# LayerNorm's inverse roots from GpSimd to ScalarE, and one of two outer products of the input weights from GpSimd to VectorE

## The chip, the cores and the metric

The kernel runs on one core of a Trainium2 chip. The metric is the device time of one execution in microseconds. Engines are called as the profile calls them: PE is TensorE's matmul and PEld its weight load, DVE is VectorE, ACT is ScalarE, POOL is GpSimd, SP is SyncE, which issues the DMAs. Each engine has its own list of instructions and takes them in the order in which the built program has them.

## What is computed

Two transformer blocks on x of 16 x 512 x 256, each with a modulated LayerNorm ahead of its two parts. The first block has a layer with fast weights and a low-rank MLP, the second has windowed attention and a channel mix.

```python
def _layernorm(x, axis=-1, eps=1e-05):
    m = jnp.mean(x, axis=axis, keepdims=True)
    v = jnp.var(x, axis=axis, keepdims=True)
    return (x - m) / jnp.sqrt(v + eps)

h = _layernorm(x, axis=-1) * (1 + ca) + sa      # and three more of this kind
```

The layer with fast weights runs over chunks of 16 tokens, one after the other. For each batch row and head it carries two matrices of 4 x 16, W_in and W_out, from chunk to chunk:

```python
def attn(q, k, v):
    s = jnp.einsum('bqhd,bkhd->bhqk', q, k) / jnp.sqrt(jnp.asarray(q.shape[-1], q.dtype))
    p = jax.nn.softmax(s, axis=-1)
    return jnp.einsum('bhqk,bkhd->bqhd', p, v)

for _ in range(2):
    g_out = -attn(W_in, k_t, v_t)
    g_in = -attn(W_out, v_t, k_t)
    W_in = W_in - lr_in * g_in
    W_out = W_out - lr_out * g_out
```

## The kernel before

The batch is cut in two halves of 8 rows, and time in 8 stretches of 64 tokens: 16 units u, whose half is u % 2. Each unit goes through five streams: `prepare` (norm a, projections, convolutions), `chain` (the recurrence, 4 chunks of 16 tokens), `mlp` (norm b), `attend` (norm c) and `mix` (norm d). They are Python generators. `timetable` (L1122) gives each of their steps a due time in units, and the steps of all units are issued in the order of those times, so that the recurrence of two units, one of each half, runs beside the other streams of earlier and later units. From what is issued the tile framework makes the order of each engine's list and the waits between engines.

`recur` (L587) is one chunk of the recurrence: 128 partitions are 8 batch rows by 16 heads. The products are made in full, as 128 x 1024 elements, on one engine, and then summed by VectorE:

- `scores` (L523) multiplies tokens and weights (sc_k, sc_q, sc_v, VectorE) and sums over d. The weights lie in `fw`, one bank of PSUM; the tokens (tok) lie in SBUF.
- `exp_tokens` (L537) takes maximum and exponential, `over_tokens` (L545) divides by the sum and multiplies with the rate (e_k, e_v, L549).
- `outer` (L530) multiplies such weights of tokens with v or k: pd_o, pd_kv and pd_i, all on POOL at L534. Both operands and the result are in SBUF. `big` (L520) gives the results one ring of five buffers.
- `total` (L634) sums a product over tokens: do and di (L636).

The two inner steps of the reference are folded together: W_in is read for the first g_out, then both gradients of W_in come from W_out at two stages, sv with 2R rows (L640 to L644). Their weights are e_v. The two products of these with k are pd_i (L647); the first sum, di0, goes into W_in at L649, which the second sc_k needs; the second, di1, follows at L653, behind that sc_k and its exponential.

The running sum over tokens, W_out at each token, is the scan at L631 (within and pd_kv, both in SBUF). Other VectorE instructions that read two operands from SBUF are mix (L1033), ov (L679), mx with mg (L900), lr (L573), and off (L353).

`norm_T` (L340) is the LayerNorm of one unit; it is called 64 times, 16 for each of a, b, c and d. VectorE takes mean and variance (mv, L348), POOL adds epsilon (L350) and raises to the power of -0.5 (L351), VectorE makes off = -mean times that root (L353), ACT applies both (xn, L359), PE transposes, and ACT applies the modulation on the way out of PSUM (L367).

ACT's table of functions is that with exponential and logarithm, except in bursts of Silu, Gelu and Tanh, around which `run` (L220) loads tables. Elsewhere `inverse_root` (L201) makes roots on ACT as Ln and Exp.

Of the kernel before, what the change touches and what calls it, by code (L numbers as in the profile page):

```python
# [12 lines left out]
AF = mybir.ActivationFunctionType  # L13
ALU = mybir.AluOpType
# [3 lines left out]
P = 128  # L18
B, T, C = 16, 512, 256
H, D, R = 16, 16, 4  # L20
CH = 16
TB = 64
HB = 8
NR = HB // 2
# [10 lines left out]
EPS = 1e-5  # L35
# [60 lines left out]
def adaln_blocks(ctx: ExitStack, tc: tile.TileContext, a: dict, out: bass.AP):  # L96
    nc = tc.nc
    mul, add, sub = ALU.mult, ALU.add, ALU.subtract
# [9 lines left out]
    def ctile(shape, name):  # L108
        return const.tile(shape, F32, tag=name, name=name)

    def bank(name):
        return ps.tile([P, 512], F32, tag="bank", name=name)
# [75 lines left out]
    nc.vector.tensor_copy(ident_bf, ident)  # L188

    w_proj = ctile([P, 2, 2, C], "w_proj")  # L190
    mhalf = ctile([P, 1], "mhalf")
    nc.vector.memset(mhalf, -0.5)

    def hold(dst, n):

# [144 lines left out]
    def norm_T(x, layer, which, b0, tag, hT):  # L340


        m = mods[layer]
        mv = work.tile([P, NR, 2], F32, tag=f"mv_{tag[0]}", name=f"mv_{tag}", bufs=1)
        for r in range(NR):
            st = work.tile([P, 6], F32, tag="st", name=f"st_{tag}_{r}", bufs=4)
            nc.vector.bn_stats(st, x[:, r, :])
            nc.vector.bn_aggr(mv[:, r, :], st)  # L348
        rs = work.tile([P, NR], F32, tag=f"rs_{tag[0]}", name=f"rs_{tag}", bufs=1)
        nc.gpsimd.tensor_scalar(rs, mv[:, :, 1], EPS, None, add)  # L350
        nc.gpsimd.tensor_tensor(rs, rs, mhalf.to_broadcast([P, NR]), ALU.pow)  # L351
        off = work.tile([P, NR], F32, tag=f"off_{tag[0]}", name=f"off_{tag}", bufs=1)
        nc.vector.scalar_tensor_tensor(off, mv[:, :, 0], -1.0, rs, mul, mul)  # L353
        for r2 in range(NR // 2):
            pt = bank(f"pt_{tag}_{r2}")
            for n in range(2):
                r = 2 * r2 + n
                xn = work.tile([P, C], F32, tag="xn", name=f"xn_{tag}_{r}", bufs=2)
                nc.scalar.activation(xn, x[:, r, :], AF.Identity, scale=rs[:, r : r + 1], bias=off[:, r : r + 1])  # L359
                for k in range(2):  # L360
                    nc.tensor.transpose(pt[:, (2 * n + k) * P : (2 * n + k + 1) * P], xn[:, k * P : (k + 1) * P], ident)
            for n in range(2):
                for k in range(2):
                    for e in range(2):
                        b = 4 * r2 + 2 * n + e
                        col = (2 * n + k) * P + e * TB
                        nc.scalar.activation(  # L367
                            hT[:, k, b, :],
                            pt[:, col : col + TB],
                            AF.Identity,  # L370
                            scale=m[:, 2 * which + 1, k, b0 + b : b0 + b + 1],
                            bias=m[:, 2 * which, k, b0 + b : b0 + b + 1],
                        )
            yield
# [19 lines left out]
    def place(u):  # L394

        return u % NH, u // NH
# [120 lines left out]
    def small(half, name, n):  # L517
        return rec.tile([P, n], F32, tag=f"s{n}_{half}", name=name, bufs={XW: 5, 2 * XW: 3}.get(n, 4))

    def big(half, name):  # L520
        return rec.tile([P, R * D * CH], F32, tag="prod", name=name, bufs=5)
# [5 lines left out]
        engine.tensor_tensor(pr, tok.unsqueeze(1).to_broadcast(every), w.unsqueeze(2).to_broadcast(every), mul)  # L527
        nc.vector.tensor_reduce(dst, pr, AX.X, add)  # L528

    def outer(half, engine, hid, tok, tag):  # L530

        pr = big(half, f"pd_{tag}").rearrange("p (r d t) -> p r d t", r=R, d=D)
        every = [P, R, D, CH]
        engine.tensor_tensor(pr, hid.unsqueeze(2).to_broadcast(every), tok.unsqueeze(1).to_broadcast(every), mul)  # L534
        return pr

    def exp_tokens(half, s, n, mx, tag):  # L537
# [7 lines left out]
    def over_tokens(half, e, n, rate, sm):  # L545

        nc.vector.tensor_reduce(sm, e, AX.X, add)
        nc.vector.reciprocal(sm, sm)
        nc.vector.scalar_tensor_tensor(e, e, rate, sm.unsqueeze(2).to_broadcast([P, n, CH]), mul, mul)  # L549
        return e  # L550
# [36 lines left out]
    def recur(u, pc, c, s):  # L587

        half = place(u)[0]
        f = fws[half]  # L590
        tag = f"{u}_{pc}_{c}"
        cs = slice(c * CH, (c + 1) * CH)
        k_dt, v_dt, q_dt, lr = s["k"][:, :, cs], s["v"][:, :, cs], s["q"][:, :, cs], s["lr"]
        lr_in, lr_out = lr[:, 0, c * CH : c * CH + 1], lr[:, 1, c * CH : c * CH + 1]
        tok = rec.tile([P, 3, CH, D], F32, tag=f"tok_{half}", name=f"tok{tag}", bufs=1)
        for n, x in enumerate((k_dt, q_dt, v_dt)):
            nc.scalar.copy(tok[:, n], x.rearrange("p d t -> p t d"))  # L597
        k, q, v = (tok[:, n] for n in range(3))
        w_in, w_out, w_outs = f["w_in"], f["w_out"], f["w_outs"]

        sc = small(half, f"scs{tag}", 2 * XW).rearrange("p (r t) -> p r t", r=R)
        scores(half, nc.vector, k, w_in, sc[:, :, :CH], f"k{tag}")
        scores(half, nc.vector, q, w_in, sc[:, :, CH:], f"q{tag}")
        late[half]()
        p_out = exp_tokens(half, sc[:, :, :CH], R, f["mx_k"], f"k{tag}")


        mx = f["hid"]
        nc.vector.tensor_reduce(mx, sc.rearrange("p r t -> p t r"), AX.X, ALU.max)
        hid = small(half, f"hid{tag}", R * 2 * CH).rearrange("p (r t) -> p r t", r=R)  # L610
        every = [P, R, 2 * CH]
        nc.vector.tensor_tensor(hid, sc, mx.unsqueeze(1).to_broadcast(every), sub)
        nc.scalar.activation(hid, hid, AF.Exp)
        yield
        d_out = outer(half, nc.gpsimd, over_tokens(half, p_out, R, lr_out, f["sm_k"]), v_dt, f"o1{tag}")

        sm = f["hid"][:, :CH]
        kh, qh = hid[:, :, :CH], hid[:, :, CH:]
        nc.vector.tensor_reduce(sm, kh.rearrange("p r t -> p t r"), AX.X, add)
        nc.vector.tensor_reduce(s["sum"][:, cs], qh.rearrange("p r t -> p t r"), AX.X, add)  # L620
        nc.vector.reciprocal(sm, sm)
        nc.vector.tensor_tensor(sm, sm, lr[:, 1, cs], mul)
        nc.vector.tensor_tensor(kh, kh, sm.unsqueeze(1).to_broadcast([P, R, CH]), mul)  # L623


        kv = outer(half, nc.gpsimd, kh, v_dt, f"kv{tag}")
        yield
        nc.vector.tensor_tensor(kv[:, :, :, 0], kv[:, :, :, 0], w_out, add)
        upto = kv
        flat = kv.rearrange("p r d t -> p (r d t)")  # L630
        nc.vector.tensor_tensor_scan(flat, within, flat, 0.0, mul, add)  # L631
        nc.vector.tensor_copy(w_outs[:, :R], upto[:, :, :, CH - 1])  # L632

        def total(pr, name):  # L634
            t = small(half, f"{name}{tag}", XW).rearrange("p (r d) -> p r d", r=R)
            nc.vector.tensor_reduce(t, pr, AX.X, add)  # L636
            return t


        sv = small(half, f"sv{tag}", 2 * XW).rearrange("p (r t) -> p r t", t=CH)  # L640
        nc.vector.tensor_tensor(w_outs[:, R:], total(d_out, "do1"), w_outs[:, :R], add)
        for n in range(2):
            scores(half, nc.vector, v, w_outs[:, n * R : (n + 1) * R], sv[:, n * R : (n + 1) * R], f"v{n}{tag}")
        p_in = exp_tokens(half, sv, 2 * R, f["mx_v"], f"v{tag}")  # L644
        yield
        p_in = over_tokens(half, p_in, 2 * R, lr_in, f["sm_v"])
        d_in = [outer(half, nc.gpsimd, p_in[:, n * R : (n + 1) * R], k_dt, f"i{n}{tag}") for n in range(2)]  # L647
        yield
        nc.vector.tensor_tensor(w_in, total(d_in[0], "di0"), w_in, add)  # L649
        sk = small(half, f"sk{tag}", XW).rearrange("p (r t) -> p r t", t=CH)  # L650
        scores(half, nc.vector, k, w_in, sk, f"k2{tag}")
        p_out = exp_tokens(half, sk, R, f["mx_k"], f"k2{tag}")
        nc.vector.tensor_tensor(w_in, total(d_in[1], "di1"), w_in, add)  # L653
        yield
        d_out = outer(half, nc.gpsimd, over_tokens(half, p_out, R, lr_out, f["sm_k"]), v_dt, f"o2{tag}")
        yield
        late[half] = lambda: nc.vector.tensor_tensor(w_out, total(d_out, "do2"), w_outs[:, R:], add)


        po = upto  # L660
        nc.gpsimd.tensor_tensor(po, qh.unsqueeze(2).to_broadcast([P, R, D, CH]), upto, mul)  # L661
        nc.gpsimd.tensor_tensor(po[:, :2], po[:, :2], po[:, 2:], add)
        nc.gpsimd.tensor_tensor(q_dt, po[:, 0], po[:, 1], add)
# [531 lines left out]
```

## Time and profile before

| | |
|---|---|
| time before, median of 3 runs | 3226.88 us (3222.9 to 3235.52) |
| time of the profiled execution | 3231.29 us |
| its span, first to last instruction | 3229.5 us |
| granted TensorE clock, mean | 0.822 |
| busy VectorE, TensorE, ACT, POOL | 2395.3, 2385.4, 1783.6, 1673.0 us |
| pd_i on POOL (L534) | 128 of 2369 ns |
| pd_o, pd_kv on POOL (L534) | 128 of 2358 ns, 64 of 2366 ns |
| inverse roots on POOL (L350, L351) | 64 of 0.23 us, 64 of 1.04 us |
| first and last start of a pd_i | 153.3 and 2956.6 us |
| table loads on ACT | 232 of 1283 ns |

A group's row in the profile has line, engine, operation, output and inputs by the program's names, their sizes, and a count; then busy us and the mean ns of one; then the engine's idle time just before them, and what ended it. A row of waits says who waited for whom: us in total, how often, and the longest. A row of one line's instructions gives minimum, median and maximum duration. What is idle is not in itself lost: it matters where the waiting engine is the one that others then wait for.

### The profile page before, as it was taken

The page shows a single profiled execution, that of the slowest core. Times are in us where ns is not written, and L with a number is a line of the kernel's source. Part 1 is how long each engine was busy: PE and PEld are TensorE (multiplying, and loading weights), DVE is VectorE, ACT ScalarE, POOL GpSimd, SP SyncE. Part 2 cuts the span into 40 slices and gives each one's busy share as a digit, 9 for nine tenths or more (in the row PEclk, how much of TensorE's full clock was granted, in tenths as well). Part 3 has the DMA queues.
Part 4 walks back from the last instruction along what each step waited for, and adds up shares of the span by engine and source line. Part 5 has one row for each costly group of instructions (what it writes and reads, how often), then busy time and mean ns, then how long its engine had stood idle before and what let it go on. Part 6 is the DMA issues. An engine that isn't in the chain of part 4 may idle for free.

```text
span 3229.5 us, 47324 instructions
## 1 busy us (share of the span) xinstructions
PE 2385.4 (74%) x17232; PEld 1452.9 (45%) x17232; DVE 2395.3 (74%) x4513; ACT 1783.6 (55%) x3748; POOL 1673.0 (52%) x1575
## 2 busy tenths in 40 slices
PE   3540156868787776887788887889787888788996
PEld 2210123444444454554445554555445555555664
DVE  1688787878787787778888888888888878774221
ACT  1761354556665745565564666566664655445543
POOL 0245556556556655555556564555555655654112
PEclk7775676878797887888888798979888887879998
DMA  5420112132314132131313223230402212122010
GB/s 151 94 58 13 47 37 67 31 73 55 80 36 94 32 83 54 51 83 33 88 27 72 69 59 75 51 83 27 100 21 72 62 51 56 45 52 60 17 28 27
DMA packets 439307, 186.46 MB, mean 58 GB/s; under 512 B 323937, under 2 KB 413090, under 8 KB 439074
## 3 DMA queue, kind: packets, MB, share of 16 engines
q1 hardware_dynamic: 439074, 183.44, 23.2%
q8 instruction: 135, 2.21, 0.3%
q14 instruction: 98, 0.80, 0.1%
HBM read 116.66 MB, written 66.72 MB: 57 GB/s over the span
## 4 chain that ended last, share of the span: by engine, by line
DVE 33%; PE 22%; POOL 20%; ACT 12%; issue 8%; DMA 4%; SPq 1%; POOLq 0%; DVEq 0%; ACTq 0%
POOL pd_o L534 5%; POOL pd_i L534 4%; DVE pd_kv L631 4%; DVE sc_v L527 3%; POOL pd_kv L534 3%; DVE sv L528 3%; DVE do L636 2%; PE st L873 2%; DVE di L636 2%; DVE sc_k L527 2%; DVE pp L460 2%; PE pproj L1005 2%; DMA oT<-o 2%; DVE scs L528 2%; DVE mx L889 1%
## 5 line engine op out<-in xcount | busy, mean ns | idle before, releaser
L534 POOL TENSOR_TENSOR pd_o<-e_k,dt_v 128x1024 f32<-128x1024 f32 x128 | 301.0, 2358 | 171.4 <-DVE e_k L549 171.3
L534 POOL TENSOR_TENSOR pd_i<-e_v,dt_k 128x1024 f32<-128x1024 f32 x128 | 298.4, 2369 | 43.4 <-DVE e_v L549 43.4
L708 PE MATMUL pwo<-w_WoT,oT 128*128 128x256 f32 x256 | 106.6, 576 | 223.0 <-POOL oT L701 201.8
L873 PE MATMUL st<-qs,keys 32*128 32x128 f32 x2048 | 191.3, 336 | 71.7 <-DVE yT L983 29.0
L661 POOL TENSOR_TENSOR pd_kv<-hid,pd_kv 128x1024 f32<-128x1024 f32 x64 | 150.3, 2349 | 165.6 <-DVE fw L632 141.6
L873 PE MATMUL sc<-keys,qs 32*128 32x128 f32 x2048 | 183.1, 326 | 71.7 <-DVE mx L889 41.7
L636 DVE TENSOR_REDUCE do<-pd_o 128x64 f32<-128x1024 f32 x126 | 152.3, 1213 | 102.5 <-POOL pd_o L534 102.5
L636 DVE TENSOR_REDUCE di<-pd_i 128x64 f32<-128x1024 f32 x128 | 155.1, 1214 | 88.3 <-POOL pd_i L534 88.3
L873 PEld LDWEIGHTS st<-qs,keys 32*128 32x128 f32 x2048 | 160.5, 226 | 132.2 <-DVE mx L889 32.4
L873 PEld LDWEIGHTS sc<-keys,qs 32*128 32x128 f32 x2048 | 148.0, 216 | 141.9 <-DVE mx L889 58.8
L889 DVE TENSOR_REDUCE mx<-sc 128x4 f32<-128x512 f32 x256 | 168.2, 679 | 26.2 <-PE sc L870 26.2
L708 PEld LDWEIGHTS pwo<-w_WoT,oT 128*128 128x128 f32 x256 | 68.4, 287 | 250.7 <-POOL oT L701 218.3
L534 POOL TENSOR_TENSOR pd_kv<-hid,dt_v 128x1024 f32<-128x1024 f32 x64 | 151.4, 2366 | 54.7 <-DVE hid L623 50.0
L926 ACT ACTIVATE pT<-st 128x512 f32<-128x512 f32 x256 | 135.3, 605 | 73.7 <-PE st L870 73.4
L631 DVE TENSOR_TENSOR_SCAN pd_kv<-within,pd_kv 128x1024 f32<-128x1024 bf16 x64 | 174.4, 2725 | 0.9
L527 DVE TENSOR_TENSOR sc_k<-tok,fw 128x1024 f32<-128x1024 f32 x128 | 155.4, 1214 | 14.8 <-ACT tok L597 13.5
L527 DVE TENSOR_TENSOR sc_v<-tok,fw 128x1024 f32<-128x1024 f32 x128 | 150.3, 1215 | 1.6
L224 ACT ACT_TABLE_LOAD x111 | 142.4, 1283 | 14.3 <-PE ph L736 7.6
L528 DVE TENSOR_REDUCE sv<-sc_v 128x64 f32<-128x1024 f32 x128 | 149.6, 1209 | 0.0
L736 PE MATMUL ph<-PT,w_v 64*128 64x512 f32 x256 | 111.1, 669 | 38.0 <-ACT z L224 27.8
L1005 PE MATMUL pproj<-w_proj,yT 128*128 128x256 f32 x512 | 122.9, 386 | 11.2 <-DVE yT L983 9.3
L197 PE MATMUL pmx<-w_w_attnT,blocks 128*128 128x384 f32 x256 | 118.5, 593 | 13.4 <-ACT hp L367 9.4
(251 smaller groups left out, 6827.7 us busy)
## 6 DMA issues: line engine op xcount, KB each, us to landing
values<-values SPq DMA_DIRECT2D x56, 256.0 KB
gate_a<-gates SPq DMA_DIRECT2D x64, 128.0 KB
xa<-in_x_dram SPq DMA_DIRECT2D x32, 256.0 KB
x<-in_x_dram SPq DMA_DIRECT2D x32, 256.0 KB
gate_c<-gates SPq DMA_DIRECT2D x64, 128.0 KB
gate_d<-gates SPq DMA_DIRECT2D x64, 128.0 KB
q<-y SPq DMA_DIRECT2D x64, 128.0 KB
dt_q<-q SPq DMA_DIRECT2D x32, 256.0 KB
```

Of the source, the lines that this page charges most:

```text
L224: ins = nc.scalar.activation(*args[0], **args[1])
L527: engine.tensor_tensor(pr, tok.unsqueeze(1).to_broadcast(every), w.unsqueeze(2).to_broadcast(every), mul)
L528: nc.vector.tensor_reduce(dst, pr, AX.X, add)
L534: engine.tensor_tensor(pr, hid.unsqueeze(2).to_broadcast(every), tok.unsqueeze(1).to_broadcast(every), mul)
L631: nc.vector.tensor_tensor_scan(flat, within, flat, 0.0, mul, add)
L636: nc.vector.tensor_reduce(t, pr, AX.X, add)
L661: nc.gpsimd.tensor_tensor(po, qh.unsqueeze(2).to_broadcast([P, R, D, CH]), upto, mul)
L708: nc.tensor.matmul(po[:, n * C : (n + 1) * C], lhsT=pair(oT, k, 2 * b2 + n), rhs=w_o[:, k, :], start=k == 0, stop=k == 1,)
L873: nc.tensor.matmul(dst, lhsT=lhsT, rhs=rhs, start=start, stop=False, skip_group_check=True)
L889: nc.vector.tensor_reduce(mx[:, j], sc[j].rearrange("p (s k) -> p s k", s=NS), AX.X, ALU.max)
L926: nc.scalar.activation(pT[j], st[j], AF.Exp)
L1005: nc.tensor.matmul(po[:, n * C : (n + 1) * C], lhsT=yT[:, k2, par].rearrange("p e t -> p (e t)"), rhs=w_proj[:, k2, par, :], start=k2 == 0 ...
```

## The change

Two things are changed. In `norm_T` the two POOL instructions of each norm, sum with epsilon and power, become two ACT instructions: Ln with epsilon as a bias, and Exp with the factor -0.5. The constant tile mhalf (-0.5) becomes eps. And `outer` takes a list of engines, between which it could divide the R rows of a product. All its callers give one engine. Of the two pd_i the first, whose sum is di0, is now given to VectorE, and the second stays on POOL. Everything else computes as before, but the order of the engines' lists is made anew for the whole program. In it the first pd_i stands directly behind its e_v on VectorE's list in 27 of 64 chunks, and one instruction later in 37.

```diff
-    mhalf = ctile([P, 1], "mhalf")
-    nc.vector.memset(mhalf, -0.5)
+    eps = ctile([P, 1], "eps")
+    nc.vector.memset(eps, EPS)
...
-        nc.gpsimd.tensor_scalar(rs, mv[:, :, 1], EPS, None, add)
-        nc.gpsimd.tensor_tensor(rs, rs, mhalf.to_broadcast([P, NR]), ALU.pow)
+        nc.scalar.activation(rs, mv[:, :, 1], AF.Ln, bias=eps)
+        nc.scalar.activation(rs, rs, AF.Exp, scale=-0.5)
...
-    def outer(half, engine, hid, tok, tag):
+    def outer(half, engines, hid, tok, tag):
 
         pr = big(half, f"pd_{tag}").rearrange("p (r d t) -> p r d t", r=R, d=D)
-        every = [P, R, D, CH]
-        engine.tensor_tensor(pr, hid.unsqueeze(2).to_broadcast(every), tok.unsqueeze(1).to_broadcast(every), mul)
+        n = R // len(engines)
+        every = [P, n, D, CH]
+        for k, engine in enumerate(engines):
+            part = slice(k * n, (k + 1) * n)
+            engine.tensor_tensor(
+                pr[:, part], hid[:, part].unsqueeze(2).to_broadcast(every), tok.unsqueeze(1).to_broadcast(every), mul
+            )
         return pr
...
-        d_in = [outer(half, nc.gpsimd, p_in[:, n * R : (n + 1) * R], k_dt, f"i{n}{tag}") for n in range(2)]
+        d_in = [
+            outer(half, engines, p_in[:, n * R : (n + 1) * R], k_dt, f"i{n}{tag}")
+            for n, engines in enumerate(([nc.vector], [nc.gpsimd]))
+        ]
```

The three other calls of `outer` (L615, L626, L655) change only from `nc.gpsimd` to `[nc.gpsimd]`.

More of the change, by code (lines that the diff above doesn't have):

```diff
@@ L614, in recur @@
         yield
-        d_out = outer(half, nc.gpsimd, over_tokens(half, p_out, R, lr_out, f["sm_k"]), v_dt, f"o1{tag}")
+        d_out = outer(half, [nc.gpsimd], over_tokens(half, p_out, R, lr_out, f["sm_k"]), v_dt, f"o1{tag}")
         sm = f["hid"][:, :CH]
@@ L623, in recur @@
         nc.vector.tensor_tensor(kh, kh, sm.unsqueeze(1).to_broadcast([P, R, CH]), mul)
-        kv = outer(half, nc.gpsimd, kh, v_dt, f"kv{tag}")
+        kv = outer(half, [nc.gpsimd], kh, v_dt, f"kv{tag}")
         yield
@@ L654, in recur @@
         yield
-        d_out = outer(half, nc.gpsimd, over_tokens(half, p_out, R, lr_out, f["sm_k"]), v_dt, f"o2{tag}")
+        d_out = outer(half, [nc.gpsimd], over_tokens(half, p_out, R, lr_out, f["sm_k"]), v_dt, f"o2{tag}")
         yield
```

## The prediction

> **What bounds it now.** I read the page's busy shares first, then its chain, then one steady stretch, then who waits for whom there.
>
> ```profile
> PE 2385.4 (74%) x17232; PEld 1452.9 (45%) x17232; DVE 2395.3 (74%) x4513; ACT 1783.6 (55%) x3748; POOL 1673.0 (52%) x1575
> ...
> DVE 33%; PE 22%; POOL 20%; ACT 12%; issue 8%; DMA 4%; SPq 1%; POOLq 0%; DVEq 0%; ACTq 0%
> ```
>
> No engine is full and no engine owns the chain. So I take two units of rows from the middle, 365.3 us in which the pattern repeats (columns: stretch, length, busy of PE, PEld, DVE, ACT, POOL, granted clock, DMA share, GB/s):
>
> ```profile
> 2028.60:2393.90 365.30, 305.23 (x2286) 186.11 (x2285) 304.84 (x564) 224.03 (x470) 204.46 (x191) 0.86 0.25 61
> ```
>
> VectorE and TensorE are both at 83 to 84%, and VectorE has 60 us left over. The waits of VectorE in that stretch sum to 30.8 us on POOL, 21.6 on ACT and 4.4 on PE. An engine takes its instructions in the built order, so its waits and its work fill the span. I therefore keep my account on VectorE's timeline: what the change adds to its work, and what it takes from its waits, over the whole run. These are its waits that the change touches (total us, times, longest):
>
> ```profile
> DVE do L636 <- POOL pd_o L534: 102.5, 63, 5.9
> ...
> DVE di L636 <- POOL pd_i L534: 88.3, 53, 4.3
> ...
> DVE off_d L353 <- POOL rs_d L351: 25.3, 16, 4.6
> DVE off_c L353 <- POOL rs_c L351: 23.6, 12, 3.5
> ...
> DVE off_a L353 <- POOL rs_a L351: 16.4, 13, 2.6
> ...
> DVE off_b L353 <- POOL rs_b L351: 5.4, 6, 1.5
> ```
>
> So POOL's outer product costs VectorE 88.3 us of waiting at di, and POOL's inverse roots 25.3 + 23.6 + 16.4 + 5.4 = 70.7 us at off. What follows the last recurrence (from 2961 us) is the same work in the same order in both programs, so the account is of the first 2960 us.
>
> **The product that moves.** One of the two pd_i of each of the 64 chunks goes from POOL to VectorE. The rows (count | busy us, mean ns | idle before):
>
> ```profile
> L534 POOL TENSOR_TENSOR pd_i<-e_v,dt_k 128x1024 f32<-128x1024 f32 x128 | 298.4, 2369 | 43.4 <-DVE e_v L549 43.4
> ...
> L527 DVE TENSOR_TENSOR sc_v<-tok,fw 128x1024 f32<-128x1024 f32 x128 | 150.3, 1215 | 1.6
> ```
>
> VectorE's product of the same size takes 1.215 us; with 0.03 us ahead of an instruction that needs the last one's result, 64 x 1.25 = +80 us of work. The wait of 88 us goes: di0 now follows its own engine. It is all di0's: between e_v and di1 stand 8.3 us of VectorE's own work in the median and 3.9 at least, beside the wait at di0 itself, against POOL's 4.7 us for both products. POOL is rid of 64 x 2.37 = 152 us.
>
> Here the price isn't only the sc_v row. sc_v reads one operand from SBUF (tok) and one from PSUM (fw). The new pd_i reads both, e_v and dt_k, from SBUF. Look at what the trace shows for such instructions beside POOL (first VectorE, then POOL, start, length):
>
> ```profile
> 2090.91 4.36 DVE L631 TENSOR_TENSOR_SCAN pd_kv<-within,pd_kv 128x1024 f32<-128x1024 bf16 x1
> ```
>
> ```profile
> 2090.78 2.34 POOL L534 TENSOR_TENSOR pd_kv<-hid,dt_v 128x1024 f32<-128x1024 f32 x1 [1.46 <-DVE hid L623]
> ```
>
> The scan takes 2.29 us in the median; here POOL had started 0.13 us ahead, and it took 4.36, that is, until POOL was through plus its own time. Its line and two others (minimum/median/maximum ns):
>
> ```profile
> L631 DVE TENSOR_TENSOR_SCAN pd_kv<-within,pd_kv x64: 2254/2291/4407, 142.2 to 2935.7; 128x1024 f32<-128x1024 bf16 x64
> ```
>
> ```profile
> L353 DVE SCALAR_TENSOR_TENSOR off_c<-mv_c,rs_c x16: 152/164/2322, 454.7 to 3074.2; 128x4 f32<-128x4 f32 x16
> ```
>
> ```profile
> L983 DVE TENSOR_TENSOR yT<-py,rs x128: 390/414/426, 541.5 to 3185.2; 128x256 f32<-128x256 f32 x128
> ```
>
> The two that read twice from SBUF spread by one POOL product; yT, with one operand in PSUM, doesn't. [...] How much it costs depends on who is first:
> - By the rows of the five other groups that read twice (L631, L1033, L679, L900, L573), mean less median times count is 28 + 16 + 13 + 12 + 7 = 75 us over 240 instructions, 0.31 us each. For 64 products: 20 us.
> [...]
>
> I choose by the order of the built program. In 27 of 64 chunks pd_i stands directly behind e_v. POOL's pd_i starts 0.08 us after e_v's end (2028.54 to 2028.62 in the timeline), VectorE's next dependent instruction after 0.03 to 0.04, so VectorE is first: 0.1 us each. In the other 37 one instruction of 0.3 to 1.1 us stands between, and POOL is first; what is left of its product is 1.2 to 2.0 us, less where POOL is still at something shorter (it sat idle ahead of a pd_i only 19 times). I take 1.2. Sum: 27 x 0.1 + 37 x 1.2 = +47 us, 0.73 us each; the ends are 20 and 138. Where POOL is second it is held up for some 1.1 us, and its pd_i1 is done about 3.6 us after e_v; di1 has 10 us of cover in the new order (5.1 at least), so that costs nothing.
>
> The cover ahead of do (work between e_k and the sum on VectorE, against the 2.5 us that POOL needs) is a little less in the new order: the shortfalls sum to 105 us instead of 89. I put +10 us.
>
> **The inverse roots.** POOL loses 64 x (0.23 + 1.04) = 81 us. ACT gets 128 instructions; its nearest rows, Ln and Exp on 128x32 (L203, L204), take 0.22 to 0.23 us: 28 us on an engine that is busy for 55%. Ln and Exp are in the table that is loaded anyway: the built program has 221 table loads instead of 232, at 1.283 us. Ln waits for VectorE's mv at the head of ACT's queue. Behind it stand copies out of PSUM, exponentials and xn, for which PE waits; before, xn stood there in the same way, waiting for off (ACT waited 154 us for it), so I put nothing for it, and bound it by +/-10 us. What VectorE waits for shrinks twice: the way is 0.5 us instead of 1.3, and in the new order 2.3 to 4.4 us of VectorE's own work (medians of the four norms) stand between mv and off, where 0.3 to 1.7 stood. By cover, 5 us of waits remain; with ACT's queue ahead of Ln I put 15. That is 55 us saved. If ACT's queue were as late as POOL was, nothing would be saved; that is the upper end.
>
> off itself gains too: its mean is 739 ns against a median of 164, 37 us over 64, because POOL starts its next product just after giving rs. Released by ACT, it should be blocked as often as the others, 0.31 us: 20 us, so -17. And POOL is 152 + 81 = 233 us less busy, 14% of 1673, so the 75 us of the other groups fall by 11.
>
> **Sum.** +80 + 47 - 88 + 10 - 55 - 17 - 11 = -34 us on VectorE's timeline. Not all of it reaches the span: ACT and PE cause 26 of the 57 us of waits in the stretch above, and those grow when VectorE comes sooner. Between 30.8/56.8 = 54% and 100%, I take 75%: -26 us. The profiled execution took 3231.3 us (span 3229.5), so 3205; against the median of 3226.9, 0.14% lower, 3201.
>
> **The rivals.**
> [...]
> - *The roots wait on ACT instead.* off's 70.7 us stay, because Ln stands behind table loads and bursts: -34 + 55 = +21, 3248. Against it is the cover in the new order. 10%.
> - *It goes nowhere.* ACT and PE, with 21.6 and 4.4 us of waits in the stretch and PE at 84%, take up all of it: 3227. 18%.
> - *The port is never lost.* VectorE is always first, and all of it arrives: -34 - 47 = -81 us, 3146. 14%.
> - *The forecast*, 3201: 40%.
>
> **How the numbers follow.** A measurement of this kernel tells 0.5%, 16 us, from no change: 3211 to 3243. The forecast's spread of some 25 us puts 0.33 of its 0.40 below 3211 and 0.07 within; with 0.14 from the last rival and 0.02 of the nil case that is 0.49 faster. Within: 0.07 + 0.15 + 0.02 = 0.24. Slower: 0.18 + 0.08 + 0.01 = 0.27. The range reaches from the port never lost, 3146, to most of the port always lost, 3272. The likeliest case alone: 3170 to 3225.
>
> **What would show it.** The pd_i row on VectorE: a mean of 1.9 us, with a maximum near 3.4, not 1.21. di's wait for POOL near nothing. L353's waits under 20 us in all, its mean under 0.5 us. The scan's and mix's means a little lower. POOL at 1440 us, VectorE near 2490. Wrong if the pd_i row's mean is over 2.5 us, if off waits over 40 us for ACT, or if do's waits rise by over 25 us.

## The result and the profile after

The changed kernel takes 3195.26 us (median of 4 runs, 3193.78 to 3203.8), the kernel before 3228.6 (4 runs). The ratio is 0.9901, 95% interval 0.9874 to 0.9928. The forecast was 3201. The profiled execution took 3203.8 us, the slowest of the four, at a span of 3201.9. So the spans of the two profiled executions differ by 27.6 us, where the medians differ by 33.3.

First the page's busy shares and its chain:

```profile
PE 2381.7 (74%) x17232; PEld 1459.1 (46%) x17232; DVE 2507.3 (78%) x4577; ACT 1790.0 (56%) x3865; POOL 1488.0 (46%) x1383
...
DVE 38%; PE 23%; POOL 13%; ACT 12%; issue 9%; DMA 4%; SPq 1%; POOLq 0%; DVEq 0%; ACTq 0%
```

VectorE works 112 us more than before, POOL 185 less. On the chain POOL went from 20 to 13% and VectorE from 33 to 38. The waits of VectorE (total us, times, longest):

```profile
DVE do L641 <- POOL pd_o L537: 122.3, 73, 3.6
...
DVE off_d L353 <- ACT rs_d L351: 6.1, 5, 2.8
...
DVE off_a L353 <- ACT rs_a L351: 0.6, 1, 0.6
DVE off_b L353 <- ACT rs_b L351: 0.6, 1, 0.6
```

The wait of di for pd_i is gone from the list, off waits for 7.3 us instead of 70.7, and do waits 20 us longer. Next the groups of the product that moved, with idle time at the end of each row:

```profile
L537 POOL TENSOR_TENSOR pd_i<-e_v,dt_k 128x1024 f32<-128x1024 f32 x64 | 176.1, 2755 | 77.9 <-DVE e_v L554 77.8
...
L537 DVE TENSOR_TENSOR pd_i<-e_v,dt_k 128x1024 f32<-128x1024 f32 x64 | 149.8, 2340 | 1.3
...
L641 DVE TENSOR_REDUCE di<-pd_i 128x64 f32<-128x1024 f32 x128 | 154.7, 1209 | 0.1
```

And the spread of its durations, minimum, median, maximum:

```profile
L537 DVE TENSOR_TENSOR pd_i<-e_v,dt_k x64: 1224/2472/3416, 151.2 to 2934.4; 128x1024 f32<-128x1024 f32 x64
```

VectorE's product takes 1.22 us at the least and 2.34 in the mean. What an instruction takes beyond its undisturbed time is called blocking here; for this row it is 64 x (2.34 - 1.22) = 72 us. All 46 of the products that took over 1.23 us ran beside an instruction of POOL. In 40 of the 64 chunks POOL's pd_i started first, and in each of them VectorE's ended 1.08 to 1.09 us after POOL's. The forecast and the expectations call this the port; the profile shows lengths, and not what in the chip makes them. The timeline shows both outcomes, in three chunks (VectorE, then POOL; start, length):

```profile
150.79 0.35 DVE L554 SCALAR_TENSOR_TENSOR e_v<-e_v,lr,fw 128x128 f32<-128x128 f32 x1
151.17 1.23 DVE L537 TENSOR_TENSOR pd_i<-e_v,dt_k 128x1024 f32<-128x1024 f32 x1
...
1290.16 0.35 DVE L554 SCALAR_TENSOR_TENSOR e_v<-e_v,lr,fw 128x128 f32<-128x128 f32 x1
1290.61 3.42 DVE L537 TENSOR_TENSOR pd_i<-e_v,dt_k 128x1024 f32<-128x1024 f32 x1
...
2016.97 0.74 DVE L1041 SCALAR_TENSOR_TENSOR mix<-hp,c_mu,mix 128x512 f32<-128x512 f32 x1
2017.63 3.36 DVE L537 TENSOR_TENSOR pd_i<-e_v,dt_k 128x1024 f32<-128x1024 f32 x1
```

```profile
151.22 3.37 POOL L537 TENSOR_TENSOR pd_i<-e_v,dt_k 128x1024 f32<-128x1024 f32 x1 [3.21 <-DVE e_v L554]
...
1290.58 2.36 POOL L537 TENSOR_TENSOR pd_i<-e_v,dt_k 128x1024 f32<-128x1024 f32 x1 [1.01 <-DVE e_v L554]
...
2017.13 2.78 POOL L537 TENSOR_TENSOR pd_i<-e_v,dt_k 128x1024 f32<-128x1024 f32 x1 [0.89 <-DVE e_v L554]
```

In the first, at 151 us, VectorE is ahead by 0.05 us, and POOL's product took 3.37 us instead of some 2.35. In the second, at 1290 us, POOL is ahead by 0.03 us, and VectorE's product took 3.42 us. In the third, at 2017 us, an instruction of mix stood between e_v and pd_i, POOL was ahead by 0.5 us, and VectorE's product took 3.36 us: it was through 1.1 us after POOL's. POOL is held up too: its own pd_i took 3.36 to 3.40 us in the 17 chunks in which VectorE's product was ahead by some 0.045 us, and 2.78 to 2.80 us in the eight in which a mix ran just before VectorE's product; the mean is 2.755 us.

### The profile page after: what moved, and what is told of

The parts are those of the page before. It is cut to its first block, busy times and chain, and to the rows that moved or that the text cites. A ratio compares the mean times of both kernels' runs of the same rounds, so it can differ in the third digit from the quotient of the medians.

```text
span 3201.9 us, 47369 instructions
## 1 busy us (share of the span) xinstructions
PE 2381.7 (74%) x17232; PEld 1459.1 (46%) x17232; DVE 2507.3 (78%) x4577; ACT 1790.0 (56%) x3865; POOL 1488.0 (46%) x1383
## 4 chain that ended last, share of the span: by engine, by line
DVE 38%; PE 23%; POOL 13%; ACT 12%; issue 9%; DMA 4%; SPq 1%; POOLq 0%; DVEq 0%; ACTq 0%
POOL pd_o L537 5%; DVE pd_kv L636 4%; DVE pd_i L537 4%; DVE sc_v L527 3%; POOL pd_kv L537 3%; DVE sv L528 3%; PE pproj L1013 2%; DVE scs L528 2%; DVE sc_k L527 2%; DVE do L641 2%; DVE di L641 2%; DVE mx L897 2%; PE ph L744 2%; DVE pp L460 2%; DMA oT<-o 1%
## 5 line engine op out<-in xcount | busy, mean ns | idle before, releaser
L881 PE MATMUL st<-qs,keys 32*128 32x128 f32 x2048 | 199.6, 337 | 72.2 <-DVE mx L897 50.2
L881 PEld LDWEIGHTS st<-qs,keys 32*128 32x128 f32 x2048 | 170.6, 227 | 128.7 <-DVE mx L897 72.5
L537 POOL TENSOR_TENSOR pd_i<-e_v,dt_k 128x1024 f32<-128x1024 f32 x64 | 176.1, 2755 | 77.9 <-DVE e_v L554 77.8
L537 DVE TENSOR_TENSOR pd_i<-e_v,dt_k 128x1024 f32<-128x1024 f32 x64 | 149.8, 2340 | 1.3
```

The costliest lines, as they stand in the source:

```text
L537: engine.tensor_tensor(pr[:, part], hid[:, part].unsqueeze(2).to_broadcast(every), tok.unsqueeze(1).to_broadcast(every), mul)
L881: nc.tensor.matmul(dst, lhsT=lhsT, rhs=rhs, start=start, stop=False, skip_group_check=True)
```

## The experiments

Each kernel was timed beside the kernel before on the same chip (medians there 3231 to 3232 us). Some expectations give theories a letter: A is the account of the forecast, part by part; B is that the product brings the gain, C that each half brings about half, and D is that the order that is made anew has a price of its own. Sums of VectorE's waits and of its busy time are of the one profiled execution of each kernel; times are medians. Nearly every edit makes the order of VectorE's list anew, too. Three pairs have nearly the same list and tell causes apart best: the roots alone and the spare roots on POOL, the changed kernel and the same with spare roots on POOL, and this last and the product alone.

**The roots alone.** In the kernel before, only L350 and L351 change, and the constant that they need; both pd_i stay on POOL.

```diff
...
-        nc.gpsimd.tensor_scalar(rs, mv[:, :, 1], EPS, None, add)
-        nc.gpsimd.tensor_tensor(rs, rs, mhalf.to_broadcast([P, NR]), ALU.pow)
+        nc.scalar.activation(rs, mv[:, :, 1], AF.Ln, bias=eps)
+        nc.scalar.activation(rs, rs, AF.Exp, scale=-0.5)
```

> The inverse roots on ScalarE alone; both pd_i stay on GpSimd. Theory A (the account on VectorE's timeline, with the rows of the changed kernel put in): the roots alone are worth 63 us of waits at off and 13 us of blocking of off, of which 75 to 100% arrive: 57 to 76 us below 3228.6, so 3153 to 3172, faster than the whole change. Theory B (the product brings the gain, since the chain is shorter and GpSimd freer, and the roots little): 3215 to 3229. Theory C (each half brings about half): 3205 to 3215.

3195.59 us, ratio 0.9888 (0.9864 to 0.9912): the same as the whole change. It lies in none of the three ranges: the roots brought more than B or C gives them, and less than A's account (3153 to 3172). The largest of VectorE's waits here:

```profile
DVE do L636 <- POOL pd_o L534: 124.9, 68, 4.7
DVE di L636 <- POOL pd_i L534: 85.8, 51, 4.5
...
DVE off_d L353 <- ACT rs_d L351: 10.2, 10, 2.8
```

The scan's rows, before and here:

```profile
L631 DVE TENSOR_TENSOR_SCAN pd_kv<-within,pd_kv 128x1024 f32<-128x1024 bf16 x64 | 174.4, 2725 | 0.9
```

```profile
L631 DVE TENSOR_TENSOR_SCAN pd_kv<-within,pd_kv 128x1024 f32<-128x1024 bf16 x64 | 186.4, 2912 | 0.8
```

off's waits fell by 59 us and its own blocking by 31. But do's waits rose by 22, and the other groups that read twice from SBUF were blocked 28 us longer: scan 12, mx 11, lr 7, ov 1, and mix 2 less. The blocking did not go, it moved to other instructions. -59 - 31 + 22 + 28 = -40 us, and the spans of the two profiled executions differ by 42: what A's account lacked is that do and the other groups take back more than half.

**The product alone.** The change without the roots; these are as in the kernel before.

```diff
...
-        d_in = [outer(half, nc.gpsimd, p_in[:, n * R : (n + 1) * R], k_dt, f"i{n}{tag}") for n in range(2)]
+        d_in = [
+            outer(half, engines, p_in[:, n * R : (n + 1) * R], k_dt, f"i{n}{tag}")
+            for n, engines in enumerate(([nc.vector], [nc.gpsimd]))
+        ]
```

> The first pd_i on VectorE alone; the inverse roots stay on GpSimd. Theory A: VectorE's busy time rises by some 131 us (64 of 2.34 us, less the overlap at both ends), 88 us of waits at di go, 20 us come at do: +63 us, of which 75 to 100% arrive: 3275 to 3292, slower than before. Theory B: 3190 to 3210. Theory C: 3205 to 3215. The mean of VectorE's pd_i is at least 2.3 us by A, because GpSimd is busier than in the changed kernel.

3274.77 us, ratio 1.0129 (1.0106 to 1.0152): 43 us slower, at the edge of what A gives. So this half of the change loses by itself, and the other half, measured on top of it, is worth 79.5 us, where it was worth 36 alone. The parts don't add.

**The product with an operand from PSUM.** The changed kernel, with 16 values of w_outs in PSUM in the place of k.

```diff
-            outer(half, engines, p_in[:, n * R : (n + 1) * R], k_dt, f"i{n}{tag}")
-            for n, engines in enumerate(([nc.vector], [nc.gpsimd]))
+            outer(half, engines, p_in[:, n * R : (n + 1) * R], tok_n, f"i{n}{tag}")
+            for n, (engines, tok_n) in enumerate((([nc.vector], w_outs[:, R : R + 1].to_broadcast([P, D, CH])), ([nc.gpsimd], k_dt)))
```

> The whole change, but the first pd_i on VectorE reads 16 values of the output weights from PSUM, repeated, in the place of k from SBUF; the first gradient of the input weights is thus another one than the reference's. It has one SBUF operand then. Theory A, port: its mean falls from 2.34 to 1.21 to 1.25 us with nothing over 1.3, GpSimd's pd_i from 2.76 back to 2.35, and of the 72 us of blocking 75 to 100% arrive: 3195 less 54 to 72, 3123 to 3141. Rival: the blocking only stands where VectorE would have waited anyway (for di1, the exponential, the other chain), and the time stays within 3180 to 3200, with other waits of VectorE larger by 50 us or more.

3192.13 us, ratio 0.9877 (0.9855 to 0.9899). The product is no longer blocked, at a mean of 1.217 us, and computes something else than the reference. The page's busy shares and chain, then the product's group:

```profile
PE 2366.1 (74%) x17232; PEld 1451.3 (46%) x17232; DVE 2435.9 (76%) x4577; ACT 1792.9 (56%) x3867; POOL 1451.8 (46%) x1383
...
DVE 32%; PE 32%; POOL 13%; ACT 12%; issue 7%; DMA 3%; SPq 1%; POOLq 0%; DVEq 0%; ACTq 0%
```

```profile
L537 DVE TENSOR_TENSOR pd_i<-e_v,fw 128x1024 f32<-128x1024 f32 x64 | 77.9, 1217 | 2.2
```

VectorE works 71 us less than in the changed kernel, and the time is 3 us less, which noise can make. Most of what was taken from VectorE came back as waits, as the rival has it: 23 us more for ACT, 23 more for PE, 4 more for POOL, and PE's share of the chain goes from 23 to 32%. The spans of these two profiled executions differ by 17 us, since that of the changed kernel was the longest of its four. And the order is another: only 3626 of 4577 instructions of VectorE stand in one order in both traces. So this is the effect of no blocking and a new order together.

**Both products on VectorE.** This takes POOL's product away from beside VectorE's, at the price of another 64 on VectorE.

```diff
-            for n, engines in enumerate(([nc.vector], [nc.gpsimd]))
+            for n, engines in enumerate(([nc.vector], [nc.vector]))
```

> The whole change, and the second pd_i on VectorE too, so that GpSimd has no pd_i. Theory A, port: it is GpSimd's pd_i, released by the same e_v, that blocks the first one: the mean of VectorE's pd_i falls to 1.5 us or less, the first 64 lose some 50 us of blocking, the second 64 add 64 x 1.25 to 1.5 = 80 to 96 us: 3195 + 30 to 46 = 3225 to 3241. Rival: GpSimd's other work blocks as much, the mean stays over 2.1 us and all of the second product comes on top: 3195 + 130 to 150, over 3320.

3222.23 us, ratio 0.9976 (0.9966 to 0.9987). The groups:

```profile
L537 DVE TENSOR_TENSOR pd_i<-e_v,dt_k 128x1024 f32<-128x1024 f32 x128 | 165.3, 1331 | 1.8
```

With no pd_i on POOL, the mean is 1.33 us, and 128 x (1.33 - 1.22) = 15 us of blocking are left of 72: most of it comes from POOL's pd_i, as A has it. The time is a little under A's range. VectorE's busy time, 2501.7 us, is no more than in the changed kernel with half as many products; the time is still 27 us longer than there. In the profiled executions VectorE waits 8 us longer for ACT, 10 for PE and 7 for POOL.

**Spare roots on ACT.** Roots made and used as before; ACT makes them too, into a tile that nobody reads. This makes the order anew (about a tenth of VectorE's list stands in another order than before) and gives ACT the new work.

```diff
...
+        ru = work.tile([P, NR], F32, tag=f"ru_{tag[0]}", name=f"ru_{tag}", bufs=1)
+        nc.scalar.activation(ru, mv[:, :, 1], AF.Ln, bias=eps)
+        nc.scalar.activation(ru, ru, AF.Exp, scale=-0.5)
```

> The roots come from GpSimd as before, and ScalarE makes them too, into a tile that nobody reads; both pd_i on GpSimd. All that is new for VectorE is an order made anew. Theory D (the three parts are: the roots, worth 79 us as between the product alone at 3274.8 and the whole change at 3195.3, which have nearly one order; a remade order of VectorE's list that costs 42 us against the one before, among it 20 us more of waits at do; and a product that costs nothing): 3250 to 3275. Rival: the order before isn't special, and the roots are worth the 37 us that they brought alone: 3225 to 3240.

3230.8 us, ratio 0.9994 (0.9984 to 1.0004). Neither the work on ACT nor this new order has a price that can be seen, so nothing speaks for theory D. It is one new order, though, and not that of the product alone.

**Spare roots on POOL.** Roots from ACT are used; POOL goes on making its own, unread. VectorE's list is that of the roots alone, but for one memset.

```diff
...
-        nc.gpsimd.tensor_scalar(rs, mv[:, :, 1], EPS, None, add)
-        nc.gpsimd.tensor_tensor(rs, rs, mhalf.to_broadcast([P, NR]), ALU.pow)
+        ru = work.tile([P, NR], F32, tag=f"ru_{tag[0]}", name=f"ru_{tag}", bufs=1)
+        nc.scalar.activation(rs, mv[:, :, 1], AF.Ln, bias=eps)
+        nc.scalar.activation(rs, rs, AF.Exp, scale=-0.5)
+        nc.gpsimd.tensor_scalar(ru, mv[:, :, 1], EPS, None, add)
+        nc.gpsimd.tensor_tensor(ru, ru, mhalf.to_broadcast([P, NR]), ALU.pow)
```

> The roots come from ScalarE as in the run with the roots alone, and GpSimd makes them too, into a tile that nobody reads; both pd_i on GpSimd. VectorE's order is that of the run with the roots alone, to the instruction. If the gain is the shorter way from mv to off: 3195 to 3210, with off's waits under 20 us; the 81 us on GpSimd are covered, but for what its power blocks of off. If the gain is that GpSimd is relieved: 3225 to 3235.

3216.97 us, ratio 0.9953 (0.9935 to 0.9972). This lies between the two ranges. By the ratios, the 36 us of the roots are 15 for the shorter way from mv to off, with the new order that comes with it, and 21 for POOL's relief. VectorE's waits, and the scan:

```profile
DVE do L641 <- POOL pd_o L539: 139.3, 67, 6.3
DVE di L641 <- POOL pd_i L539: 87.2, 53, 4.5
```

```profile
L636 DVE TENSOR_TENSOR_SCAN pd_kv<-within,pd_kv 128x1024 f32<-128x1024 bf16 x64 | 186.4, 2912 | 0.8
```

off's waits had fallen by 61 us here too, but do's stand at 139.3 instead of 102.5: 22 us of this rise were there with the roots alone, 14 came with POOL's spare work. That VectorE, released earlier at off, comes to do before POOL is through fits this, but no run shows it apart. (The profiled execution was 10 us above the median.) The blocking is telling: POOL works 86 us more than with the roots alone, and scan, mix, mx and lr are blocked exactly as long, to within 0.2 us; ov is blocked 8 us less.

**The first product left out.** The changed kernel without the first pd_i and its sum di0; W_in gets the weights e_v instead.

```diff
-            for n, engines in enumerate(([nc.vector], [nc.gpsimd]))
+            for n, engines in ((1, [nc.gpsimd]),)
...
-        nc.vector.tensor_tensor(w_in, total(d_in[0], "di0"), w_in, add)
+        nc.vector.tensor_tensor(w_in, p_in[:, :R], w_in, add)
...
-        nc.vector.tensor_tensor(w_in, total(d_in[1], "di1"), w_in, add)
+        nc.vector.tensor_tensor(w_in, total(d_in[0], "di1"), w_in, add)
```

> The whole change, with the first pd_i and its sum di0 left out: the 64 weights themselves are added to the input weights in the place of the sum. VectorE has some 131 + 75 us less to do, GpSimd keeps its one pd_i, and the chain loses both steps. If VectorE's timeline sets the time as the prediction had it, 75 to 100% of 206 us arrive: 2990 to 3040. If the limit is elsewhere (the changed kernel without its 72 us of blocking gained 3), less than half arrives: over 3095, with VectorE's waits for ScalarE and TensorE together up by over 80 us.

3086.64 us, ratio 0.955 (0.9525 to 0.9575).

```profile
PE 2364.1 (77%) x17232; PEld 1460.5 (47%) x17232; DVE 2292.4 (74%) x4449; ACT 1776.0 (58%) x3859; POOL 1463.1 (47%) x1383
```

VectorE works 2507.3 - 2292.4 = 215 us less, and 3195.3 - 3086.6 = 109 us arrive, half: between the two expectations, and nearer to the second, the limit elsewhere. Waits for ACT grew by 67 us, for PE by 19.

**The product alone, with an operand from PSUM.** The edit of the third experiment, with the roots on POOL.

> The product alone on VectorE (roots on GpSimd), with 16 repeated values from PSUM in the place of k, so that its gradient is another than the reference's. The blocking of VectorE's pd_i is gone. If blocking is part of the 42 us that the product alone cost: 3274.8 less 54 to 72, 3203 to 3221. If it is made up by other waits, as in the run with both parts: 3255 to 3275.

3211.99 us, ratio 0.9936 (0.9912 to 0.996). The durations of its product:

```profile
L537 DVE TENSOR_TENSOR pd_i<-e_v,fw x64: 1195/1220/1222, 152.9 to 2932.5; 128x1024 f32<-128x1024 f32 x64
```

Not one of the 64 was blocked. VectorE works 61 us less than with the product alone, and 63 us arrive. The same blocking, taken from the changed kernel, brought 3. Here too the order is another than with the product alone: 3966 of 4577 instructions of VectorE stand in one order.

**The changed kernel with spare roots on POOL.** The edit of the sixth experiment, on the changed kernel; VectorE's list is the changed kernel's but for one memset.

> The changed kernel, in which POOL also makes the 64 inverse roots, as before the change, into a tile that nobody reads; everything that is used still comes from ACT. VectorE's list is the same as in the changed kernel but for one memset, and nearly the same as in the kernel with the product alone (3275 us). Between the two lie 79.5 us that the roots are worth once a product is on VectorE. Theory of the shorter way: nearly all of it comes from off getting its root earlier (off waits 7 instead of 60 us); POOL's 81 us of spare work give back no more than the 21 us that they gave back with both products on POOL: 3205 to 3217. Rival, relief of POOL: in this order POOL's roots stand ahead of its own products and are what delays pd_o, pd_kv and x; then most of the 79.5 us is given back, 3250 to 3275, with VectorE's waits for POOL at 200 us or more instead of 162.

3190.05 us, ratio 0.9873 (0.9852 to 0.9894). Giving POOL its roots back, 92 us of busy time, costs nothing here: the time is under the range of the first theory, and the interval overlaps that of the changed kernel. VectorE's waits:

```profile
DVE do L646 <- POOL pd_o L542: 135.8, 74, 3.8
...
DVE off_d L358 <- ACT rs_d L353: 4.6, 5, 1.9
```

Against the product alone, whose list on VectorE is nearly the same (4361 of 4577 instructions of the traces stand in one order) and whose POOL has the same work, the time is 85 us less. In the two profiled executions VectorE's waits at off fell by 55 us, its other waits for ACT by 19, those for PE by 13 and its busy time by 13; other waits for POOL rose by 14, 11 of them at do. This is nearly all of it: -55 - 19 - 13 - 13 + 14 = -86, where the spans differ by 87. Once a product is on VectorE, the whole worth of the roots lies in their being made on ACT, the shorter way, and none in POOL's relief.

**The first product divided.** Two of its four rows on each of the two engines, which `outer` allows.

```diff
-            for n, engines in enumerate(([nc.vector], [nc.gpsimd]))
+            for n, engines in enumerate(([nc.vector, nc.gpsimd], [nc.gpsimd]))
```

> The changed kernel with the first product pd_i divided by rows: two of four on VectorE, two on POOL, which then makes the second product whole. Account as in the forecast: VectorE's work falls by 64 x 0.6 = 38 us, and blocking should fall too, since VectorE's half takes 0.65 us; but di0 must again wait for POOL's half (some 1.2 us from e_v, beside 0.65 us on VectorE), and pd_i1 comes 1.2 us later. Theory: since taking 71 us from VectorE's work in the changed kernel brought only 3 us, this brings no more than 10: 3185 to 3200. Rival: the shorter product and a shorter blocking arrive as they did with roots on POOL (63 of 61 us), and 38 us or more arrive: 3150 to 3165. Third possibility: di0 waits again as it did before (88 us, some 40 at half the length), and the time is 3205 to 3225.

3181.01 us, ratio 0.9833 (0.9809 to 0.9857), 14 us less than the changed kernel; the two intervals do not meet. Against the kernel with spare roots, timed beside it, it is 9 us less, and there the intervals just overlap. The groups, then the waits:

```profile
L537 POOL TENSOR_TENSOR pd_i<-e_v,dt_k 128x512 f32<-128x512 f32 x64 | 100.9, 1577 | 45.4 <-DVE e_v L554 45.4
...
L537 DVE TENSOR_TENSOR pd_i<-e_v,dt_k 128x512 f32<-128x512 f32 x64 | 66.5, 1039 | 1.5
```

```profile
DVE do L641 <- POOL pd_o L537: 99.2, 54, 4.4
...
DVE di L641 <- POOL pd_i L537: 53.4, 47, 2.9
```

VectorE works 75 us less than in the changed kernel; 53 of it come back as waits of di, and do waits 23 us less. The theory's range ended at 3185, a little too high.

**The other products divided.** Roots on ACT, both pd_i on POOL, and the two pd_o of each chunk divided (the second, o2, in the same way as the first).

```diff
-            for n, engines in enumerate(([nc.vector], [nc.gpsimd]))
+            for n, engines in enumerate(([nc.gpsimd], [nc.gpsimd]))
...
-        d_out = outer(half, [nc.gpsimd], over_tokens(half, p_out, R, lr_out, f["sm_k"]), v_dt, f"o1{tag}")
+        d_out = outer(half, [nc.vector, nc.gpsimd], over_tokens(half, p_out, R, lr_out, f["sm_k"]), v_dt, f"o1{tag}")
...
```

> Roots on ACT, both pd_i on POOL, and instead the two products pd_o of each chunk divided by rows between VectorE and POOL, since do's wait for pd_o was the largest of VectorE's waits in nearly all kernels (102 to 139 us). It adds 128 x 0.65 = 83 us to VectorE's work and takes 128 x 1.2 = 150 us from POOL's. Theory: do's wait shrinks to less than 40 us, but the work and the blocking at the port that go with it are as large, and the time stays near that of the roots alone: 3185 to 3215. Rival: do's wait ends the path where others don't, and 40 us or more arrive: under 3160. Second rival: VectorE is first at the port for its half, so that POOL's half comes later and do's wait stays over 80 us: 3230 to 3260.

3254.71 us, ratio 1.0065 (1.0047 to 1.0083). The time is the second rival's, its wait is not:

```profile
DVE di L641 <- POOL pd_i L537: 102.5, 57, 4.3
DVE do L641 <- POOL pd_o L537: 58.6, 54, 3.5
```

do's wait halved, 66 us less than with the roots alone, but VectorE's busy time rose by 87 us, di waits 17 us longer, and waits for ACT rose by 38. Taking 66 us from the largest wait in the list cost more than it brought.

## Why the prediction was right, and which of its steps were not

The time was right, within 6 us, and so were the signs of the two halves: the product alone loses and the roots alone gain. But several terms were off, in both directions, and that they came to nearly the right sum is in part luck.

- **The product's work**, +80: the moved product's unblocked time is 64 x 1.22 = 78 us. Right.
- **The blocking**, +47: mis-sized, 72 by the row. The forecast split the chunks by the built order, and the split held for most. Of the 27 chunks in which pd_i follows e_v directly, 18 took 1.22 us, with POOL starting some 0.045 us later in nearly all of them. In 4, POOL was first by 0.025 us and VectorE took about 3.4 us; in 5, POOL was still at an earlier instruction. The mean is 0.40 us, not 0.1. In the 4, the trace has two semaphores (by which it shows one engine waiting for another) for pd_i to wait for, VectorE's own and POOL's, and pd_i started 0.104 us after e_v; in the 18 it has one, and pd_i started after 0.034 us. POOL started some 0.08 us after e_v in both. The forecast took the shorter start for all 27. In the other 37 all were blocked by 0.1 us or more, by 1.66 us in the mean, not 1.2. I had put what is left of POOL's product at 1.2 to 2.0 us and taken the lower end; but in 26 of the 37 the instruction between was short, some 0.4 to 0.75 us (1.2 in two), and POOL's product was only 0.1 to 0.5 us old when VectorE's started. 27 x 0.40 + 37 x 1.66 = 72. At 1.13 us a product it stayed just under the 1.26 us (the 0.73 of the sum, and its gain of 34 us over 64 products) from which the forecast's own account gives a loss. The end of 138 us that stands beside the sum is shown by no run: the longest of the 64 products took 2.19 us more than the shortest, and all together were blocked for 72 us.
- **di's waits**, -88: right, they are gone.
- **do's waits**, +10: 20, below the 25 that I had set as a limit. They rose to 112 to 139 us in the changed kernel and in eight of the eleven experiments.
- **off's waits**, -55: 63. ACT has the roots in time, as the cover in the built order said; the rival of roots waiting on ACT is out.
- **off's own blocking**, -17: -13, because off_d now meets POOL more often: 11 of its 16 start while POOL is at an instruction, where 3 did before, and its row's median is 1610 ns, where the other three have 137 to 152. **The other groups that read twice**, -11: -6. mix is blocked 12 us less and ov 7, but mx, lr and the scan 13 longer. The reason, that blocking falls with POOL's busy time, didn't hold: in the roots alone POOL works 84 us less, and these groups are blocked 28 us longer; with POOL's spare roots added to that kernel, in the same order, they are blocked 8 us less, and with the same added to the changed kernel 13 us less. More work on POOL did not mean more blocking; that it depends on which instructions meet is what remains, and is argued. POOL's relief was itself mis-sized: its busy time fell by 185 us, not 233, 25 of the difference because its pd_i now takes 2.755 us. (Its roots took 87 us, not 81: the 0.23 us of the sum with epsilon is a median, the mean is 0.32.)
- **The sum and the 75%.** The listed terms, as measured, give 150 - 88 + 20 - 63 - 13 - 6 = 0 us, not -34. The span fell by 27.6 nevertheless. 18 us of it are time that two records of VectorE share: the rows' sum rose by 130 us, the busy time by 112, for the record of one instruction can start before that of the one before it ends, as that of pd_i at 2017.63 us does in the lines above, by 0.08 us. 12 are waits for POOL elsewhere, and 8 waits for PE; waits for ACT other than off's took 16 back; the rest lies in short gaps and small rows. So most of the gain between these two executions lies where the forecast had not counted it: this is the luck in its total. The 75% is not confirmed. Where VectorE's work was cut, with the order made anew, the part that arrived was 3 of 71 us, 109 of 215, and 63 of 61.

What the forecast didn't have at all is that the two halves depend on each other. The times in us, by where the roots are made and where the first product:

| first pd_i | roots on POOL | roots on ACT | difference |
|---|---|---|---|
| on POOL | 3232 | 3195.6 | 36 |
| on VectorE | 3274.8 | 3195.3 | 79.5 |
| on VectorE, operand from PSUM | 3212.0 | 3192.1 | 20 |

The forecast's terms for the product alone, 80 + 47 - 88 + 10 = +49, agree with the +43 measured where the roots are on POOL. Where they are on ACT, it costs nothing. The forecast's terms for the roots, -55 - 17 and part of -11, lie between the first two values of the right column. So the sum fits one way through the table: first the product, with the roots on POOL (+43), then the roots, with the product on VectorE (-79.5). By the other way, the roots first (-36) and then the product (nothing), its terms fit neither step. The halves don't add.

The experiments with spare roots show that, with both products on POOL, the shorter way was worth 15 us, a new order included, and POOL's relief another 21; with one product off POOL, the shorter way was worth 85 and the relief nothing. A reading that fits: POOL has room in the second case and not in the first, where waits saved at off are partly given back at do (37 us more of 61, in the sixth experiment; 11 of 55 in the ninth). That the one causes the other is argued, not shown. Why taking away the blocking on VectorE is worth 63 us with late roots and 3 with early ones stays open. The two kernels with the PSUM operand give the sizes, but no single wait that explains the difference, and their orders differ from those of the kernels that they are held against; how much of it is the order was not tested.

For the kernel itself: the product on VectorE adds nothing that the roots alone don't bring; dividing it between the two engines is the best of what was tried that computes the same.

## What to carry to other kernels

Test the halves of a change alone: here one gave all of the gain and the other, alone, was a loss, and neither could be seen in the sum. When an operation that reads two operands from SBUF moves from GpSimd to VectorE, count what else the same producer releases on GpSimd, and look in the built order at what stands between. Here the product took 1.22 us where it started 0.045 us ahead of GpSimd's; where GpSimd's had started first, in 40 of 64 chunks, it ended 1.08 us after that one, so that such a meeting is to be priced at nearly all that is left of GpSimd's instruction. An edit that moves an operation also makes the order anew: a kernel in which the old work goes on beside the new, unread, can keep the list nearly as it is and so tell the two apart. A wait near the top of the list isn't what it costs: look at what is late next, by taking the wait away while all other work stays.

## What the runs showed of the hardware

- Some hundredths of a microsecond decided which of the two products was long: VectorE's took 1.22 us where it started 0.045 us ahead of POOL's, and about 3.4 us where it started 0.025 us behind, for the same instruction behind the same producer. The four chunks of the second kind are among the 6 of the 27 in which VectorE's product had two semaphores to wait for. It started 0.104 us after e_v in all 6, and 0.034 us in all 21 with one; in two of the four POOL's earlier work had ended a microsecond before.
- The blocking costs both sides: POOL's pd_i took up to 3.40 us instead of some 2.35 when VectorE was first, and 2.755 in the mean. With an operand in PSUM instead, none of the 64 products took over 1.222 us beside the same pd_i on POOL, and POOL's took 2.811 us at most (the product alone, roots on POOL).
- Blocking didn't follow POOL's busy time: with POOL busy for 1588.8 us (roots alone) the scan's row was 186.4 us, with 1675.2 us in the same order (spare roots on POOL) also 186.4, and before, with 1673.0 us, 174.4.
